# A cross-attention kernel on one core: a new order of all engines and transfers, other softmax forms for seven groups, and the last product, sum and store in halves

## The chip, the core and the metric

The kernel runs on one core of a Trainium2 chip. The engines are TensorE (PE in the profile; its weight loads are PEld), VectorE (DVE), ScalarE (ACT), GpSimd (POOL) and SyncE (SP), which here only issues transfers. Each engine works through its own queue in order, and semaphores hold an instruction until what it needs is done. The metric is the device time of one execution in microseconds (us); the median of three runs before the change is 498.08 (498.07 to 498.1).

## The reference

Everything is float32. With x of 2 batches x 2048 tokens x 640 channels, and a context of 2 x 154 tokens x 1024 channels, of which 77 are text and 77 image prompt:

```python
q = _split_heads(hidden_states @ Wq.T, H)          # 20 heads of 32
k = _split_heads(text @ Wk.T, H)
v = _split_heads(text @ Wv.T, H)
out_text = _merge_heads(_attend(q, k, v, sm_scale))
k_ip = _split_heads(ip @ Wk_ip.T, H)
v_ip = _split_heads(ip @ Wv_ip.T, H)
out_ip = _merge_heads(_attend(q, k_ip, v_ip, sm_scale))
out = out_text + IP_SCALE * out_ip                 # IP_SCALE = 1
out = out @ Wo.T + bo
return out + residual
```

`_attend` is a softmax of the scaled scores times the values. So there are two softmaxes of 77 keys for each token and head, an output projection, and a residual.

## The kernel before

**Tiling.** All inputs come transposed, with the contracted dimension first. The 640 channels are five chunks of 128, of four heads each. Work is numbered by a unit u = 0 to 19, a half (1024 tokens) of one chunk of one batch; q = u // 2 counts batch and chunk, so units 0 to 9 are batch 0 and 10 to 19 batch 1. Within a unit the scores come in three groups s = 0, 1, 2 of three, three and two tiles of 128 tokens. A group's scores lie as rows of 154 (text and image keys side by side), four heads to a tile, in the big buffer `pb`.

**The order by hand.** The function that issues the instructions does nothing but walk a string of words, `SCHEDULE`, in order (before 1024 words, now 1031). Each word puts its instructions at the end of the queues of the engines that it uses, so the order of the words is the order on each engine; the framework only adds the semaphores. `@n` in a word names the PSUM bank or buffer to use. The words that matter below, with their engine and line before the change:

- `q.u.h`, `cq.u.h`: queries of 512 tokens (PE, L201) and their copy out (ACT, L211). `k`, `v`, `ck`, `cv`: the same for keys and values (PE, L142).
- `R s.u`: the scores of a group (PE, L233). `K`: copy to `pb` (ACT, L245). `M`: row maxima (DVE, L281, or L284 from the bank). `S`: subtract them (POOL, L295). `E`: exponential (ACT, L301 in one piece, L269 row by row). `D`: row sums (DVE, L306). `I`: reciprocal (DVE, L311). `N`: normalise (POOL, L316). `T`: transpose by 32x32 blocks (DVE, L323). `A.q`: weights times values (PE, L332), `CA.q` its copy (ACT).
- `m i.x`, `cm i.x`: the output projection of batch 0 in seven products for each 512 tokens x (PE, L490 and L500), and their sums into `acc` (DVE, L515 and L521). Two products share a bank (`m6` uses that of `m1`): the first must be added before the second is written. `o`, `co`, `p`, `z`, `yz`: the last output chunk. `G`: sums of operands for the products (POOL, L431). `SF`, `SS`: fetch and store a part of `acc` (SP).
- Batch 1's output projection is a scheme of 33 products. `V.w.j.e` is a step of the sum of weights w (L828 or L826), `X.w.e` a sum of tokens (L834), each on DVE (e = d) or POOL (e = p). `F m.h`: product m for the 512 tokens h (PE, L848). `Y c.h.t`: adds what lies in the bank of chain c into an output part (DVE, L792 for the first, L794 after), and after the part's last add its store is issued (SP, L798).
- `LX`, `LQ`, `LK`, `LW`, `LA`: loads (SP).

**Softmax forms.** A plain group takes K, M, S, E, D, I, N, T. A group in `BIASED` has no S: the exponential runs row by row, 24 or 16 times, with the negated maximum as bias. A group in `DIRECT` also has no K: maxima and exponential read the banks. A group in `SUMMED` has no D: each row's exponential also sums, and each such sum costs a read instruction on ScalarE.

Of the kernel before, what the change touches and what calls it, by code (L numbers as in the profile page):

```python
# [9 lines left out]
F32 = mybir.dt.float32  # L10
# [10 lines left out]
def kernel(  # L21
# [25 lines left out]
    nc = tc.nc  # L47
    P = 128
# [16 lines left out]
        (11, 0), (13, 0), (13, 2), (14, 0), (14, 2), (15, 1), (15, 2), (16, 2), (18, 1),  # L65
    }
    BIASED = {
        (2, 2), (3, 2), (4, 2), (5, 2), (6, 2), (7, 2), (9, 2), (11, 2), (12, 0), (12, 2), (18, 2), (19, 0),
        (19, 2),
    }  # L70
    SUMMED = {
        (4, 2), (6, 2), (11, 2), (12, 0), (12, 2), (13, 0), (13, 2), (14, 0), (15, 1), (15, 2), (18, 1),
        (18, 2), (19, 2),
# [480 lines left out]
    for t in range(2):  # L554
# [233 lines left out]
    def add_part(o, ps, op):  # L788
# [7 lines left out]
        if not parts_left[o]:  # L796
            m, i = o
            nc.sync.dma_start(out=outT[ts(m, P), ds(S + i * TB, TB)], in_=t)  # L798
# [92 lines left out]
```

## Time and profile before

| | |
|---|---|
| median of three runs | 498.08 us |
| profiled execution: span | 496.7 us |
| busy: PE, DVE, ACT, POOL | 490.3, 408.5, 315.0, 362.5 us |
| granted TensorE clock | 1.00 in every stage |
| DMA | 69.38 MB, 140 GB/s in the mean |

The profiled execution's span runs from its first to its last recorded instruction; a run's time is some 1.4 us longer than this span. A row of a timeline gives its start, its length, engine, line, operation, output and inputs, shapes and how many instructions were joined, and in brackets how long the engine had been idle and what released it. A row of a group gives busy time, mean ns of one, and the idle time before.

### The profile page before, as it was taken

To read this page: it belongs to the slowest core of one execution; us is meant where nothing else is said; L and a number is where in the kernel's file an instruction comes from. 1 tells how busy PE (TensorE), PEld (TensorE's weight loads), DVE (VectorE), ACT (ScalarE), POOL (GpSimd) and SP (SyncE) were. 2 spreads that over 40 slices of the span, in tenths; PEclk is the share of its full clock that TensorE was granted. 3 is DMA by queue.
4 is the path that set the end of the run, shared out by engine and by line. 5 is a ranking of instruction groups with operands and counts; after the bars stand their busy time and mean duration, and the time that the engine had idled before them with its cause. 6 is when DMAs were issued, how large, how long until landed. Compare 5 with 4: busy or idle time off the path is not lost.

```text
span 496.7 us, 10482 instructions
## 1 busy us (share of the span) xinstructions
PE 490.3 (99%) x4114; PEld 287.9 (58%) x4114; DVE 408.5 (82%) x412; ACT 315.0 (63%) x1021; POOL 362.5 (73%) x157
## 2 busy tenths in 40 slices
PE   8999999999999999999999999999999999999997
PEld 5676657657547556456647654755755675444442
DVE  0069989979979989969976896687999978898877
ACT  1165878978978778668999786587578966100000
POOL 0069978798888999989874858565899888284830
PEclk9999999999999999999999999999999999999999
DMA  8991440332360454886445177418525401420115
GB/s 259 356 246 40 132 120 1 106 93 69 92 213 3 132 178 132 274 273 237 158 152 191 58 244 210 133 57 246 174 69 171 127 23 43 149 84 1 43 73 223
DMA packets 67474, 69.38 MB, mean 140 GB/s; under 512 B 5473, under 2 KB 47201, under 8 KB 67425
## 3 DMA queue, kind: packets, MB, share of 16 engines
q1 hardware_dynamic: 66704, 68.00, 43.8%
q8 instruction: 32, 0.52, 0.5%
q10 hardware_dynamic: 720, 0.72, 0.4%
q14 instruction: 18, 0.14, 0.1%
HBM read 54.94 MB, written 10.49 MB: 132 GB/s over the span
## 4 chain that ended last, share of the span: by engine, by line
PE 92%; DMA 3%; SPq 1%; DVE 1%; POOL 1%; ACT 1%; issue 0%; POOLq 0%
PE bank L201 33%; PE bank L848 11%; PE bank L490 10%; PE bank L233 10%; PE bank L332 10%; PE bank L142 9%; PE bank L471 6%; PE bank L500 3%; DMA aT<-in_L_xattn_Wk_ip_dram 2%; DMA wq<-in_L_xattn_Wq_dram 2%; SPq L534 1%; POOL pb L316 1%; DVE den L306 0%; ACT pb L301 0%; SPq L132 0%
## 5 line engine op out<-in xcount | busy, mean ns | idle before, releaser
L316 POOL TENSOR_TENSOR pb<-pb,rden 128x1848 f32<-128x1848 f32 (+1 forms) x60 | 176.1, 2944 | 39.7 <-DVE rden L311 35.5
L201 PE MATMUL bank<-x,wq 128*128 128x512 f32 x400 | 180.4, 601 | 0.6 <-DMA x<-in_x_dram 0.5
L295 POOL TENSOR_TENSOR pb<-pb,mx 128x1848 f32<-128x1848 f32 (+1 forms) x38 | 119.3, 3152 | 51.8 <-DVE mx L281 51.5
L201 PEld LDWEIGHTS bank<-x,wq 128*128 128x128 f32 x400 | 74.1, 191 | 86.7 <-issue 80.8
L323 DVE STREAM_TRANSPOSE pb<-pb 128x1920 f32<-128x1920 f32 (+1 forms) x60 | 115.7, 1932 | 4.9 <-POOL pb L316 4.3
L281 DVE TENSOR_REDUCE mx<-pb 128x24 f32<-128x1848 f32 (+1 forms) x51 | 93.7, 1850 | 30.7 <-ACT pb L245 30.5
L245 ACT COPY pb<-bank 128x462 f32<-128x462 f32 (+1 forms) x204 | 87.2, 539 | 36.0 <-PE bank L233 35.4
L306 DVE TENSOR_REDUCE den<-pb 128x24 f32<-128x1848 f32 (+1 forms) x47 | 88.7, 1895 | 17.6 <-ACT pb L301 13.3
L301 ACT ACTIVATE pb<-pb 128x1848 f32<-128x1848 f32 (+1 forms) x38 | 64.2, 1696 | 17.8 <-POOL pb L295 17.5
L269 ACT ACTIVATE pb<-pb,mx 128x77 f32<-128x77 f32 x224 | 67.8, 364 | 0.3 <-DVE mx L281 0.2
L233 PEld LDWEIGHTS bank<-kT,qT 32*128 32x128 f32 x1280 | 45.4, 184 | 26.9 <-issue 15.6
L269 ACT ACTIVATE pb<-bank,mx 128x77 f32<-128x77 f32 x184 | 51.8, 386 | 9.3 <-DVE mx L284 9.3
L233 PE MATMUL bank<-kT,qT 32*128 32x154 f32 x1280 | 56.2, 305 | 0.3 <-ACT kT L559 0.3
L332 PE MATMUL bank<-pb,v 32*32 32x512 f32 x1600 | 55.2, 597 | 0.0
L142 PE MATMUL bank<-wo_ct,aT 128*128 128x154 f32 x320 | 45.6, 296 | 0.3 <-DMA aT<-in_L_xattn_Wk_ip_dram 0.3
L142 PEld LDWEIGHTS bank<-wo_ct,aT 128*128 128x128 f32 x320 | 42.9, 188 | 3.6 <-issue 2.2
L332 PEld LDWEIGHTS bank<-pb,v 32*32 32x32 f32 x1600 | 29.9, 103 | 22.8 <-issue 10.7
L211 ACT ACTIVATE qT<-bank 128x512 f32<-128x512 f32 x40 | 24.2, 619 | 22.1 <-PE bank L201 22.0
L471 PE MATMUL bank<-aT,wo_ct 128*128 128x512 f32 x80 | 36.1, 596 | 0.0
L269 ACT ACTIVATION_READ_ACCUMULATOR pb<-bank,mx 128x1 f32 x128 | 33.6, 267 | 0.0
L490 PE MATMUL bank<-aT,wo_ct 128*128 128x256 f32 x128 | 32.3, 385 | 0.0
L490 PEld LDWEIGHTS bank<-aT,wo_ct 128*128 128x128 f32 x128 | 23.7, 190 | 6.5 <-issue 3.0
(75 smaller groups left out, 434.4 us busy)
## 6 DMA issues: line engine op xcount, KB each, us to landing
x<-in_x_dram SPq DMA_DIRECT2D x20, 1280.0 KB, 6.7
out_dram<-acc SPq DMA_DIRECT2D x20, 256.0 KB, 2.3
x<-in_x_dram SPq DMA_DIRECT2D x18, 256.0 KB, 5.9
acc<-in_x_dram SPq DMA_DIRECT2D x16, 256.0 KB, 4.7
out_dram<-x SPq DMA_DIRECT2D x15, 256.0 KB, 2.0
v<-vS SPq DMA_DIRECT2D x160, 20.0 KB, 2.8
wq<-in_L_xattn_Wq_dram SPq DMA_DIRECT2D x9, 320.0 KB, 5.0
aT<-in_L_xattn_Wk_dram SPq DMA_DIRECT2D x5, 512.0 KB, 5.5
```

The costliest lines, as they stand in the source:

```text
L142: nc.tensor.matmul(keys_in(out), loaded[n][:, k, :], cT[:, k, :, t, :], start=(k == 0), stop=(k == NCC - 1))
L201: nc.tensor.matmul(pq, wqs[q % 3][:, k, :], xs[place_of(u, h)][:, k, :], start=(k == 0), stop=(k == NC - 1),)
L233: nc.tensor.matmul(ps[g][:, ts(t, 2 * L)], qTs[(u, h)][g * D : (g + 1) * D, ts(st, P)], kT[g * D : (g + 1) * D, c, b].rearrange("p t l -> ...
L245: nc.scalar.copy(keys_of(u, s)[:, :, g], ps[g][:, : n * 2 * L].rearrange("p (n l) -> p n l", n=n))
L269: nc.scalar.activation(row, row if ps is None else rows_in(ps[g], n)[:, t, x], AF.Exp, bias=maxs[(u, s)][:, *one], accum_out=None if den i ...
L281: nc.vector.tensor_reduce(mx, rows_of(u, s), AX.X, ALU.max, negate=negate)
L295: nc.gpsimd.tensor_tensor(rows_of(u, s), rows_of(u, s), maxs[(u, s)].unsqueeze(3).to_broadcast([P, n, 2, L]), ALU.subtract)
L306: nc.vector.tensor_reduce(den_of(u, s), rows_of(u, s), AX.X, ALU.add)
L316: nc.gpsimd.tensor_tensor(rows_of(u, s), rows_of(u, s), rdens[(u, s)].unsqueeze(3).to_broadcast([P, n, 2, L]), ALU.mult)
L323: nc.vector.transpose(p, p)
L332: nc.tensor.matmul(pa[r][g * D : (g + 1) * D, :], v4s[q % 2][rows, g, k, :], zones[rows, :, g, k, :], start=(k == 0), stop=(k == NK - 1),)
L490: nc.tensor.matmul(part, w_of[m][:, kp, op], t_of(m, b, i)[:, kp], start=(op == kp == 0 and m in (1, 2, 5)), stop=(op == 1 and kp == 1 and ...
```

## The change

1. Three sets of forms change. `DIRECT` loses (14, 0) and gains (12, 0); `BIASED` loses (12, 0), (18, 2), (19, 0) and gains (10, 0); `SUMMED` loses (4, 2), (13, 0), (13, 2), (14, 0), (18, 2). Each pair is (unit, group). Gone from the order are S0.10 and K0.12; new are D2.4, D0.13, D2.13, K0.14, S0.14, D0.14, S2.18, D2.18 and S0.19.
2. The whole of `SCHEDULE` is in another order, transfers included.
3. `CLOSING` names product F6.1 and the add Y0.1.10. The product is issued as two matmuls of 256 columns, and the add as two halves, each with its own store.
4. The places of the resident blocks (`home`) are worked out ahead, so that `LA` can stand later in the order.

The diff, cut to its core (of the order, the lines spoken of later):

```diff
     DIRECT = {
-        (11, 0), (13, 0), (13, 2), (14, 0), (14, 2), (15, 1), (15, 2), (16, 2), (18, 1),
+        (11, 0), (12, 0), (13, 0), (13, 2), (14, 2), (15, 1), (15, 2), (16, 2), (18, 1),
     }
     BIASED = {
-        (2, 2), (3, 2), (4, 2), (5, 2), (6, 2), (7, 2), (9, 2), (11, 2), (12, 0), (12, 2), (18, 2), (19, 0),
-        (19, 2),
+        (2, 2), (3, 2), (4, 2), (5, 2), (6, 2), (7, 2), (9, 2), (10, 0), (11, 2), (12, 2), (19, 2),
     }
     SUMMED = {
-        (4, 2), (6, 2), (11, 2), (12, 0), (12, 2), (13, 0), (13, 2), (14, 0), (15, 1), (15, 2), (18, 1),
-        (18, 2), (19, 2),
+        (6, 2), (11, 2), (12, 0), (12, 2), (15, 1), (15, 2), (18, 1), (19, 2),
     }
...
-        "CA.8 G7.3 T2.18 m5.3@0 V.P.0.d K1.19 V.D.0.d V.P.1.d V.I.0.p V.Q.0.d X.B.p@2 m1.3@2 M1.19 V.K.0.p R0.19@1 "
+        "E2.18 D2.18 R1.19@1 V.P.0.d CA.8 m5.3@0 I2.18 SS.2.2 SF.3.2 N1.18 K1.19 SS.3.4 m1.3@3 N2.18 X.B.p@2 V.P.1.d "
+        "V.Q.0.d G6.3 T1.18 SS.2.3 VS.9.0 M1.19 cm5.3 S1.19 T2.18 R0.19@1 K0.19 M0.19 S0.19 E1.19 SF.3.3 m2.3@2 V.T.0.d "
...
+        "F23.0 F26.1@0 F30.0 X.X.p@r31 Y0.0.01 Y6.1.21 F23.1 X.Q.p@10 Y2.1.31 Y2.0.31 V.F.0.p F30.1 F13.0 Y2.1.21 "
+        "Y7.1.21 Y7.0.21 F24.0 F2.1 V.W.1.d F2.0 F15.1 X.O.d@2 Y6.0.20 Y7.1.11 F13.1 F8.0 X.P.p@13 Y7.0.11 X.J.d@4 "
+        "Y6.1.20 X.K.p@1 F5.1 F8.1 Y7.1.31 X.F.p@r21 F5.0 F15.0 Y6.0.30 Y2.1.11 Y7.0.31 F27.1 F27.0 F1.0 Y2.0.11 "
...
+    CLOSING = (6, 1), (0, 1, "10")
+
+    def add_part(o, ps, op, cut=1):
+        whole, n = sum_at(o), TB // cut
+        fresh = o in untouched
+        untouched.discard(o)
+        parts_left[o] -= 1
+        for z in range(cut):
+            add_columns(o, whole[:, ts(z, n)], ps[:, ts(z, n)], op, fresh, z * n)
+
+    def add_columns(o, t, ps, op, fresh, first):
+        if fresh:
             nc.vector.scalar_tensor_tensor(t, t, bo_sb[:, o[0] : o[0] + 1], ps, ALU.add, op)
         else:
             nc.vector.tensor_tensor(t, t, ps, op)
         if not parts_left[o]:
             m, i = o
-            nc.sync.dma_start(out=outT[ts(m, P), ds(S + i * TB, TB)], in_=t)
+            nc.sync.dma_start(out=outT[ts(m, P), ds(S + i * TB + first, t.shape[-1])], in_=t)
...
-            nc.tensor.matmul(
-                at[(c, h)], weight(w), tokens_of(x)[:, h], start=first, stop=True, skip_group_check=True
-            )
+            cut = 2 if (m, h) == CLOSING[0] else 1
+            for z in range(cut):
+                cols = ts(z, TB // cut)
+                nc.tensor.matmul(
+                    at[(c, h)][:, cols], weight(w), tokens_of(x)[:, h, cols], start=first, stop=True,
+                    skip_group_check=True,
+                )
```

How the order moves instructions is shown at three places. In these listings a row is a line, an operation, and its output and inputs; the changed kernel's line numbers differ by a few (L316 is now L314, L323 L321, L281 L279, L515 L513, L828 L829, L826 L827, L834 L835, L794 L798, L848 L852).

**VectorE and GpSimd behind attention A.8.** VectorE before, from I2.18 (T1.18, T2.18, then V.P.0 and V.D.0, V.P.1, V.Q.0, M1.19, cm5.3, cm2.3):

```order
L311 RECIPROCAL rden_2_3506<-den_2_3400 128x16
L323 STREAM_TRANSPOSE pb<-pb 128x1920
L323 STREAM_TRANSPOSE pb<-pb 128x1280
L828 TENSOR_TENSOR pb<-wo_ct 128x128 x2
L828 TENSOR_TENSOR pb<-pb,wo_ct 128x128
L826 SCALAR_TENSOR_TENSOR pb<-pb,wo_ct 128x128
L281 TENSOR_REDUCE mx_1_3554<-pb 128x24
L515 SCALAR_TENSOR_TENSOR acc<-bank_67,bo_sb,acc 128x256 x2
L515 SCALAR_TENSOR_TENSOR acc<-bank_70,bo_sb,acc 128x256 x2
```

VectorE now, from D2.18 (then V.P.0, I2.18, V.P.1, V.Q.0, T1.18, M1.19, cm5.3, T2.18, M0.19, V.T.0):

```order
L304 TENSOR_REDUCE den_2_3488<-pb 128x16
L829 TENSOR_TENSOR pb<-wo_ct 128x128
L309 RECIPROCAL rden_2_3513<-den_2_3488 128x16
L829 TENSOR_TENSOR pb<-pb,wo_ct 128x128
L827 SCALAR_TENSOR_TENSOR pb<-pb,wo_ct 128x128
L321 STREAM_TRANSPOSE pb<-pb 128x1920
L279 TENSOR_REDUCE mx_1_3542<-pb 128x24
L513 SCALAR_TENSOR_TENSOR acc<-bank_67,bo_sb,acc 128x256 x2
L321 STREAM_TRANSPOSE pb<-pb 128x1280
L279 TENSOR_REDUCE mx_0_3564<-pb 128x24
L829 TENSOR_TENSOR pb<-pb,wo_ct 128x128
```

The two transposes have moved from ahead of the weight sums to behind them, I2.18 stands between V.P.0 and V.P.1, and a sum D2.18 is new.

GpSimd before, from N1.18 (N2.18, G7.3, V.I.0, X.B, V.K.0):

```order
L316 TENSOR_TENSOR pb<-pb,rden_1_3417 128x12x154
L316 TENSOR_TENSOR pb<-pb,rden_2_3506 128x8x154
L431 TENSOR_TENSOR aT<-aT 128x2x256
L828 TENSOR_TENSOR pb<-pb,wo_ct 128x128
L834 TENSOR_TENSOR aT<-aT 128x1024
L828 TENSOR_TENSOR pb<-wo_ct,pb 128x128
```

GpSimd now, from S2.18 (N1.18, N2.18, X.B, G6.3, S1.19):

```order
L293 TENSOR_TENSOR pb<-pb,mx_2_3396 128x8x154
L314 TENSOR_TENSOR pb<-pb,rden_1_3480 128x12x154
L314 TENSOR_TENSOR pb<-pb,rden_2_3513 128x8x154
L835 TENSOR_TENSOR aT<-aT 128x1024
L429 TENSOR_TENSOR aT<-aT,x_85 128x2x256
L293 TENSOR_TENSOR pb<-pb,mx_1_3542 128x12x154
```

N2.18 has come from ahead of the weight sums to the row that follows I2.18, the subtraction S2.18 is new, and V.I.0 and V.K.0 have moved to a later place.

**VectorE and GpSimd in the last stage.** VectorE now, from the add Y2.1.21 (Y7.1.21, Y7.0.21, V.W.1, X.O, Y6.0.20, Y7.1.11, Y7.0.11, X.J, Y6.1.20):

```order
L798 TENSOR_TENSOR x_83<-x_83,bank_72 128x512
L798 TENSOR_TENSOR x_83<-x_83,bank_67 128x512
L798 TENSOR_TENSOR x_84<-x_84,bank_74 128x512
L829 TENSOR_TENSOR pb<-pb,wo_ct 128x128
L835 TENSOR_TENSOR aT<-pb 128x1024
L796 SCALAR_TENSOR_TENSOR acc<-acc,bo_sb,bank_68 128x512
L798 TENSOR_TENSOR x_83<-x_83,bank_67 128x512
L798 TENSOR_TENSOR x_84<-x_84,bank_74 128x512
L835 TENSOR_TENSOR pb<-aT 128x1024
```

GpSimd now, from X.L (X.X, X.Q, V.F, X.P, X.K, X.F):

```order
L835 TENSOR_TENSOR pb<-aT,pb 128x1024
L835 TENSOR_TENSOR aT<-aT 128x2x512
L835 TENSOR_TENSOR pb<-aT,pb 128x1024
L829 TENSOR_TENSOR pb<-wo_ct 128x128
L835 TENSOR_TENSOR pb<-pb,aT 128x1024
L835 TENSOR_TENSOR x_85<-aT,pb 128x1024
L835 TENSOR_TENSOR aT<-aT 128x2x512
```

GpSimd before, from X.P (X.L, X.V, X.K, X.Q, V.R.1, X.N):

```order
L834 TENSOR_TENSOR pb<-pb,aT 128x1024
L834 TENSOR_TENSOR pb<-aT,pb 128x1024
L834 TENSOR_TENSOR pb<-aT 128x1024
L834 TENSOR_TENSOR x_85<-aT,pb 128x1024
L834 TENSOR_TENSOR pb<-aT,pb 128x1024
L828 TENSOR_TENSOR pb<-pb,wo_ct 128x128
L834 TENSOR_TENSOR pb<-x_85,pb 128x1024
```

On GpSimd X.P has moved from ahead of X.L to behind X.X and X.Q. On VectorE the weight sum V.W.1 and the token sum X.O now stand back to back ahead of the adds that empty chain 6's banks.

**The end.** TensorE before:

```order
L848 MATMUL bank_71<-pb,wo_ct 128x512
L848 MATMUL bank_73<-pb,wo_ct 128x512
L848 MATMUL bank_67<-aT,pb 128x512
L848 MATMUL bank_67<-pb,wo_ct 128x512
```

TensorE now:

```order
L852 MATMUL bank_67<-aT,pb 128x512
L852 MATMUL bank_67<-pb,wo_ct 128x512
L852 MATMUL bank_73<-aT,pb 128x256 x2
L852 MATMUL bank_73<-pb,wo_ct 128x512
```

VectorE now, its last adds:

```order
L798 TENSOR_TENSOR acc<-acc,bank_67 128x512
L798 TENSOR_TENSOR x_84<-x_84,bank_70 128x512
L798 TENSOR_TENSOR x_82<-x_82,bank_73 128x256 x2
```

The halved product F6.1 stands last but one; the last, F18.1, is whole, and the two half-adds read its bank.

More of the change, by code (lines that the diff above doesn't have):

```diff
@@ L786, in sum_at @@
         return acc[:, m] if m < NC - 1 else res
-    def add_part(o, ps, op):
-        t = sum_at(o)
-        if o in untouched:
-            untouched.discard(o)
+    CLOSING = (6, 1), (0, 1, "10")
[8 more added lines that the diff above has]
+        if fresh:
             nc.vector.scalar_tensor_tensor(t, t, bo_sb[:, o[0] : o[0] + 1], ps, ALU.add, op)
@@ L794, in add_part @@
             nc.vector.tensor_tensor(t, t, ps, op)
-        parts_left[o] -= 1
         if not parts_left[o]:
             m, i = o
-            nc.sync.dma_start(out=outT[ts(m, P), ds(S + i * TB, TB)], in_=t)
-    home = {}
+            nc.sync.dma_start(out=outT[ts(m, P), ds(S + i * TB + first, t.shape[-1])], in_=t)
+    home = {step_of(u)[3] * NH + h: xs[place_of(u, h)] for u, h in late[-XROOM:]}
     def finish(k, args, where):
@@ L809, in finish @@
         elif k == "LA":
-            for u, h in late[-XROOM:]:
-                home[step_of(u)[3] * NH + h] = xs[place_of(u, h)]
             (fourth,) = set(range(NHB)) - set(home)
@@ L847, in finish @@
             w, x = PRODUCTS[m].split()
-            nc.tensor.matmul(
-                at[(c, h)], weight(w), tokens_of(x)[:, h], start=first, stop=True, skip_group_check=True
-            )
+            cut = 2 if (m, h) == CLOSING[0] else 1
[5 more added lines that the diff above has]
+                )
         elif k[0] == "Y":
             c, h, t = int(k[1:]), int(args[0]), args[1]
-            add_part((int(t[0]), NH * int(t[1]) + h), at[(c, h)], sign_of[(c, t)])
+            add_part(
+                (int(t[0]), NH * int(t[1]) + h), at[(c, h)], sign_of[(c, t)], 2 if (c, h, t) == CLOSING[1] else 1
+            )
         else:
```

118 rows, old and new, of the table SCHEDULE are left out of this document.

## The prediction

> **What bounds the kernel now.** I read the page first (busy time, chain of waits), then the table by stages, then the waits of TensorE.
>
> ```profile
> span 496.7 us, 10482 instructions
> PE 490.3 (99%) x4114; PEld 287.9 (58%) x4114; DVE 408.5 (82%) x412; ACT 315.0 (63%) x1021; POOL 362.5 (73%) x157
> ...
> PE 92%; DMA 3%; SPq 1%; DVE 1%; POOL 1%; ACT 1%; issue 0%; POOLq 0%
> ```
>
> TensorE is busy for 490.3 of 496.7 us and carries 92% of the chain that ended last. No other engine is full over the span. The stages say where its missing time lies, and how close the next engine is:
>
> ```profile
> 0.00:24.40 24.40, 22.29 (x76) 13.44 (x76) 0.17 (x1) 3.69 (x8) 0.83 (x6) 1.00 0.96 306
> ...
> 346.30:388.70 42.40, 42.40 (x396) 26.11 (x400) 40.26 (x38) 31.48 (x100) 38.54 (x17) 1.00 0.45 138
> ...
> 442.20:496.70 54.50, 50.80 (x119) 21.93 (x117) 43.83 (x66) 0.00 (x0) 25.23 (x12) 1.00 0.23 87
> ```
>
> The columns are length, PE, PEld, DVE, ACT, POOL, clock, DMA share, GB/s. TensorE idles 2.1 us in the start, which waits for the first loads, and 3.7 us in the last stage, nearly all of it behind its last product. Between them it is full. VectorE has only 2.1 us to spare from 346.30 to 388.70, and that is the engine whose lateness would show next. The waits that the profile names are small:
>
> ```profile
> PE bank L201 <- DMA x<-in_x_dram: 0.5, 1, 0.5
> ...
> PE bank L490 <- DVE acc L515: 0.2, 1, 0.2
> ```
>
> So three things can change the time: TensorE's own work, the small hand-offs inside it, and what stands behind the last product. A new order can win little and lose anything.
>
> **TensorE's work: 0.** Both programs have the same score, query, attention and output products. One of 128x512 becomes two of 128x256, with equal columns. The same groups of scores and of attention stand between the other products, only in another sequence, so I count no work gained or lost.
>
> **Hand-offs: -0.5 (-1.1 to +0.2).** Where TensorE is a little held up, a row is longer than its like, or the gap to it is:
>
> ```profile
> 58.07 1.80 PE L233 MATMUL bank<-kT,qT 32*128 32x154 f32 x40
> ...
> 80.63 1.59 PE L233 MATMUL bank<-kT,qT 32*128 32x154 f32 x40
> ...
> 311.10 1.07 PE L233 MATMUL bank<-kT,qT 32*128 32x154 f32 x24
> 312.41 1.13 PE L490 MATMUL bank<-aT,x 128*128 128x256 f32 x4 [0.24 <-DVE acc L515]
> ...
> 406.42 0.59 PE L500 MATMUL bank<-aT,x 128*128 128x256 f32 x2
> 407.13 1.97 PE L490 MATMUL bank<-aT,x 128*128 128x256 f32 x8
> ```
>
> Forty scores take 1.80 us at 58.07 and 1.59 us at 80.63: 0.21 lost. At 312.41 another 0.24 goes. The two products of 406.42 need about 0.44 by the rate of the row behind them (1.97 for eight), so they are through at 406.86, and the next begin at 407.13: about 0.27 goes. There are ten such places, 2.6 us in all by the same reading. In the new order the scores after q.3.0 have a key or value projection ahead of them, and the row of 312.41 follows other work: these two and a like one go (0.7), and I find two new ones of 0.1 to 0.2 where a projection follows attention. That is -0.5; the bounds are three more gone, and three more new. The hand-off at 407.13 is dealt with below.
>
> **The end in halves: -0.3 (-0.45 to +0.1).**
>
> ```profile
> 493.03 0.69 DVE L794 TENSOR_TENSOR acc<-acc,bank 128x512 f32<-128x512 f32 x1 [0.41 <-PE bank L848]
> 493.75 0.33 SPq L798 DMA_DIRECT2D out_dram<-acc  x1
> ```
>
> ```profile
> out_dram<-acc SPq DMA_DIRECT2D x20, 256.0 KB, 2.3
> ...
> L515 DVE SCALAR_TENSOR_TENSOR acc<-bank,bo_sb,acc 128x256 f32<-128x256 f32 x32 | 13.7, 468 | 7.0 <-PE bank L500 7.0
> ```
>
> Behind the last product stand one add of 0.69, one issue and the flight of 256 KB, some 3.7 us to the end. In the change the product that is cut, F6.1, is the last but one; F18.1 is last and whole and writes the bank that both half-adds read. So the cut of the product gains nothing. The two half-adds cost about 0.4 each (the 256-column add of L515, 0.47, has three operands) in place of 0.69: the second ends 0.1 later, while the first half's store is under way and the last flight carries 128 KB. If half of the flight of 2.3 us were size, it would save 0.6; two issues of 0.33 follow one another and the fixed part stays. I take -0.3, nearer to the issue row than to the size. It costs +0.1 if the flight is all latency.
>
> **The forms: 0.**
>
> ```profile
> L269 ACT ACTIVATION_READ_ACCUMULATOR pb<-bank,mx 128x1 f32 x128 | 33.6, 267 | 0.0
> ```
>
> ```profile
> L306 DVE TENSOR_REDUCE den<-pb 128x24 f32<-128x1848 f32 x35 | 72.1, 2060 | 14.0 <-ACT pb L301 13.3 <-ACT pb L269 0.6
> ...
> L306 DVE TENSOR_REDUCE den<-pb 128x16 f32<-128x1232 f32 x12 | 16.9, 1412 | 3.6 <-ACT pb L269 3.6
> ```
>
> Five groups no longer sum on ScalarE: 96 reads of up to 0.27, some 26 us less there. VectorE gets five sums back, 2 x 2.06 + 3 x 1.41 = 8.4 us over 490. Neither engine is the bound; they lie beside TensorE's products. The cover is thin only where VectorE is nearly full, and there (D2.18, 1.41) T1.18 and T2.18 have been moved behind it. That is the next term.
>
> **The turn of V.Q: +1.4 (0 to +2.4).** Two rows of one stretch show who gets in where VectorE leaves a gap between two sums:
>
> ```profile
> 392.20 2.26 POOL L316 TENSOR_TENSOR pb<-pb,rden 128x1232 f32<-128x1232 f32 x1 [0.42 <-DVE rden L311]
> ...
> 396.46 0.46 POOL L828 TENSOR_TENSOR pb<-pb,wo_ct 128x128 f32<-128x128 f32 x1 [0.77 <-DVE pb L828]
> ```
>
> ```profile
> 396.30 0.28 DVE L828 TENSOR_TENSOR pb<-pb,wo_ct 128x128 f32<-128x128 f32 x1
> 396.61 0.45 DVE L826 SCALAR_TENSOR_TENSOR pb<-pb,wo_ct 128x128 f32<-128x128 f32 x1
> ...
> 472.73 1.50 DVE L828 TENSOR_TENSOR pb<-pb,wo_ct 128x128 f32<-128x128 f32 x1
> ```
>
> ```profile
> 469.41 4.66 POOL L834 TENSOR_TENSOR aT<-aT 128x1024 f32<-128x1024 f32 x2
> ```
>
> V.Q.0 must wait for V.P.1, and in this gap (396.58 to 396.61) GpSimd's V.I.0, asked for at 396.46, got in: V.Q.0 took 0.45, not 0.28. At 472.73 a VectorE sum of 0.28 took 1.50: it ended at 474.23, just behind GpSimd's pair of sums (469.41 + 4.66 = 474.07). So the two engines hold one another out with such two-input instructions. In the new order V.Q.0 has the same gap, but what GpSimd has ready is N2.18, which waits for I2.18, the row before V.P.1. N2.18 is the 2.26 us kind. No row of before has a normalisation against a weight sum: it could hold V.Q.0 for nothing, or for its 2.26 less 0.15. It has the operation and the two SBUF inputs of the sums that do hold, so I take the latter.
>
> The Trainium skill ("SBUF — State Buffer", section "Who interferes with whom") says that a VectorE instruction with two SBUF inputs contends with a GpSimd one that reads SBUF, and whoever issues first has the shared pair for the whole instruction. By it N2.18 holds V.Q.0 too, and the term is the same 1.4; without it the term is 0. The row of 472.73 agrees, with 1.50 for 0.28.
>
> What is late next goes by these rows:
>
> ```profile
> 388.72 5.47 PE bank L332 x153
> ```
>
> ```profile
> 384.77 1.38 DVE L281 TENSOR_REDUCE mx<-pb 128x16 f32<-128x1232 f32 x1
> ...
> 390.43 0.71 DVE L481 SCALAR_TENSOR_TENSOR res<-bank,bo_sb,res 128x512 f32<-128x512 f32 x1
> ```
>
> ```profile
> L316 POOL TENSOR_TENSOR pb<-pb,rden 128x1848 f32<-128x1848 f32 x40 | 131.3, 3288 | 24.8 <-DVE rden L311 22.7 <-ACT aT L355 1.1 <-ACT pb L245 0.6
> ```
>
> ```profile
> L323 DVE STREAM_TRANSPOSE pb<-pb 128x1920 f32<-128x1920 f32 x40 | 86.3, 2160 | 3.7 <-POOL pb L316 3.2
> ...
> L281 DVE TENSOR_REDUCE mx<-pb 128x24 f32<-128x1848 f32 x35 | 71.5, 2051 | 28.4 <-ACT pb L245 28.3
> L323 DVE STREAM_TRANSPOSE pb<-pb 128x1280 f32<-128x1280 f32 x20 | 29.5, 1477 | 1.2 <-POOL pb L316 1.2
> ...
> L521 DVE TENSOR_TENSOR acc<-acc,bank 128x512 f32<-128x512 f32 x12 | 7.9, 662 | 0.8 <-PE bank L490 0.8
> ```
>
> T1.17 must be ready when attention A.8 starts, about 388.4 (388.72 less the hand-offs gone). VectorE being nearly full, I put its end at 387.4 (386.5 to 388.4). Then come co.3 (0.7) and M2.18 (1.4): 389.5. On GpSimd follow S2.18 (2.25, as 392.20), N1.18 (3.29) and, with hops of 0.1 and the row I2.18 between, N2.18 from 395.5 to 397.8; V.Q.0 ends at 398.0. Behind it on VectorE stand T1.18 2.16, M1.19 2.05, cm5.3 2 x 0.47, T2.18 1.48, M0.19 2.05, V.T.0 0.28, cm2.3 2 x 0.47 and cm1.3 0.66: 10.6, less 0.08 of overlap at each of ten: 9.8. cm1.3 ends at 407.8. It empties the bank that m6.3 writes, and m6.3's place on TensorE is 407.13 - 0.27 - 0.5 = 406.4. It is 1.4 late. Without the lost turn V.Q.0 ends 2.1 sooner and m6.3 is on time.
>
> **The turn of V.W.1: +1.8 (0 to +3.9).** In the last stage GpSimd gets four long instructions in a row, X.X, X.Q, V.F, X.P, and then X.K. VectorE comes to V.W.1 and X.O seven adds after F23.0.
>
> ```profile
> L834 DVE TENSOR_TENSOR pb<-aT 128x1024 f32<-128x1024 f32 x7 | 8.3, 1221 | 1.7 <-PE bank L332 1.5 <-ACT aT L359 0.2
> ```
>
> ```profile
> 440.08 0.49 DVE L828 TENSOR_TENSOR pb<-pb,wo_ct 128x128 f32<-128x128 f32 x2
> ...
> 440.13 1.16 POOL L828 TENSOR_TENSOR pb<-wo_ct 128x128 f32<-128x128 f32 x2
> ```
>
> From the end of X.D, X.P is asked for after 2.33 + 2.33 + 0.46 = 5.1 us. F23.0 ends some 0.5 to 1.2 after X.D (my count of the rows between them; both hang on the same adds), and seven adds of 0.6 to 0.7 bring VectorE to V.W.1 after 4.7 to 6.1: mostly behind X.P. Then V.W.1, and X.O, Y6.0.20, Y7.1.11, Y7.0.11, X.J and Y6.1.20 behind it, wait up to 2.3 us, and X.J once more for X.K, which X.O has held out. Y6.0.20 and Y6.1.20 empty the banks of F8.0 and F8.1, ten and twelve products of 0.86 after F23.0. Counted out, with X.O and X.J at 1.2 and adds at 0.6, the slack of 0.9 to 2 us takes part of the first wait and F8.1 is late by about 1.8. If VectorE is first, the cost is 0. If GpSimd's X.K gets in ahead of X.O as well, it is another 2.1, 3.9 in all. The row of 440.08 speaks for the middle: two sums on VectorE back to back kept GpSimd out (two of 0.41 to 0.46 took 1.16).
>
> **Sum:** 0 - 0.5 - 0.3 + 0 + 1.4 + 1.8 = +2.4 on the span of 496.7, so 499.1. The median before, 498.08, is 1.4 above its span, hence **500.5**.
>
> **The rivals.**
> *The turns hold*: normalisation doesn't hold V.Q.0, and V.W.1 comes first. Then -0.8: 497.3. For it: V.W.1 and X.P are within 0.7 us of one another, and nothing shows N against V. Against it: the row of 472.73.
> *Only V.Q's turn is lost*: -0.8 + 1.4: 498.7. For it: the same nearness at V.W.1.
> *X.O's turn goes too*: -0.8 + 1.4 + 3.9 = +4.5: 502.6. By the rule of the Trainium skill named above, X.K, asked for during V.W.1, would come first, which gives this. The row of 440.08 is against it; by that row GpSimd, having asked, was kept out.
> *Transfers late*: stores and fetches of the parts of batch 0 share SP's queue in a new order; the closest fetch has about 2 us in hand, and one of 4.7 us median that misses costs 1 to 2 us: about 499 with no turn lost. DMA is at 0.45 in the busiest of the later stages quoted.
>
> **How the numbers follow.** Forecast 0.30, turns hold 0.27, only V.Q 0.20, X.O too 0.18, transfers 0.05. Less than 0.2%, 1.0 us, can't be told from no change here: faster is below 497.1, slower above 499.1. Turns held spreads from 496.6 to 498.3, half of it faster: 0.14. Same takes its other half, and most of "only V.Q" and of the transfers: 0.32. Slower is the rest, 0.54. The range, 497.0 to 502.8, leaves out half of the faster cases and the worst of the last one; the forecast's own is 499.3 to 501.7.
>
> **What would show it.** Right: V.Q.0 takes over 2 us, and m6.3 begins over 1 us after the product before it; V.W.1 takes over 2 us and F8.1 waits. F18.1 is followed by two adds and two issues, with under 3.7 us to the end. Wrong: V.Q.0 at 0.3 to 0.5 with N2.18 beside it; V.W.1 ahead of X.P; or TensorE idle at a place that I have not named, a product of batch 0 that waits for a fetched part above all.

## The result, and the profile after

The changed kernel takes **502.47 us** (median of four runs, 502.22 to 504.02) where the kernel before took 498.07 beside it: slower by 4.4 us, or by a factor of 1.0088. The ratio on record, 1.0101 with a 95% interval of 1.0085 to 1.0116, is higher, as the mean of the four runs is, with the one of 504.02 among them. The page of the changed kernel, whose span is 500.7 us:

```profile
PE 490.4 (98%) x4116; PEld 287.5 (57%) x4116; DVE 425.8 (85%) x418; ACT 299.9 (60%) x887; POOL 371.6 (74%) x159
...
PE 86%; DVE 7%; DMA 3%; SPq 1%; issue 1%; ACT 1%; POOL 0%; ACTq 0%; DVEq 0%
```

TensorE's own work is the same (490.3 before), and VectorE, which had 1% of the chain that ended last, now has 7%. The table by stages and the waits of TensorE say where:

```profile
388.70:423.70 35.00, 34.66 (x304) 22.83 (x287) 34.01 (x38) 17.52 (x51) 32.38 (x17) 1.00 0.20 60
...
442.20:500.70 58.50, 51.34 (x121) 22.29 (x119) 48.40 (x68) 0.00 (x0) 25.72 (x14) 0.99 0.23 86
```

```profile
PE bank L852 <- DVE acc L796: 2.2, 1, 2.2
PE bank L852 <- DVE x L796: 1.3, 1, 1.3
```

In the last stage TensorE idles 7.2 us (58.50 less 51.34); it was 3.7. The two waits are F8.0 and F8.1. Here is the place, first VectorE (V.W.1, X.O, Y6.0.20), then GpSimd (X.P, X.K), then TensorE (F8.0, F8.1):

```profile
452.99 2.13 DVE L829 TENSOR_TENSOR pb<-pb,wo_ct 128x128 f32<-128x128 f32 x1
455.04 3.36 DVE L835 TENSOR_TENSOR aT<-pb 128x1024 f32<-128x1024 f32 x1
458.32 0.74 DVE L796 SCALAR_TENSOR_TENSOR acc<-acc,bo_sb,bank 128x512 f32<-128x512 f32 x1
```

```profile
452.62 2.36 POOL L835 TENSOR_TENSOR pb<-pb,aT 128x1024 f32<-128x1024 f32 x1
454.92 2.41 POOL L835 TENSOR_TENSOR x<-aT,pb 128x1024 f32<-128x1024 f32 x1
```

```profile
459.12 1.12 PE L852 MATMUL bank<-aT,pb 128*128 128x512 f32 x2 [2.21 <-DVE acc L796]
...
462.42 1.13 PE L852 MATMUL bank<-aT,pb 128*128 128x512 f32 x2 [1.32 <-DVE x L796]
```

V.W.1, alone some 0.28 us, takes 2.13: it ends at 455.12, just behind X.P (454.98). X.O, alone 1.2, takes 3.36: it ends at 458.40, after X.K (457.33) and its own 1.1. X.K had been asked for at 454.92, X.O at 455.04. So both turns were lost.

The other place, VectorE (V.P.0, V.Q.0), GpSimd (N1.18, N2.18) and TensorE (m6.3):

```profile
393.64 0.80 DVE L829 TENSOR_TENSOR pb<-wo_ct 128x128 f32<-128x128 f32 x1
...
394.88 2.27 DVE L827 SCALAR_TENSOR_TENSOR pb<-pb,wo_ct 128x128 f32<-128x128 f32 x1
```

```profile
391.00 3.29 POOL L314 TENSOR_TENSOR pb<-pb,rden 128x1848 f32<-128x1848 f32 x1
394.75 2.25 POOL L314 TENSOR_TENSOR pb<-pb,rden 128x1232 f32<-128x1232 f32 x1 [0.46 <-DVE rden L309]
```

```profile
407.21 1.97 PE L488 MATMUL bank<-aT,x 128*128 128x256 f32 x8 [0.34 <-DVE acc L519]
```

V.P.0 ends at 394.44, behind N1.18 (394.29), and V.Q.0 at 397.15, behind N2.18 (397.00). Normalisation does hold VectorE. Yet m6.3 waits only 0.34. The reason stands just before, in attention A.8 (TensorE), where its weight loads find nothing to issue, while SP has sent two transfers of 256 KB at A.8's start:

```profile
387.78 6.47 PE L330 MATMUL bank<-pb,v 32*32 32x512 f32 x160
```

```profile
393.21 0.13 PEld L330 LDWEIGHTS bank<-pb,v 32*32 32x32 f32 x2 [0.81 <-issue]
```

```profile
387.69 0.37 SPq L459 DMA_DIRECT2D acc<-in_x_dram  x1
388.15 0.42 SPq L463 DMA_DIRECT2D out_dram<-res  x1
```

A.8 takes 6.40 us from its start to that of the scores behind it; it took 5.48 before. The end:

```profile
497.11 0.75 DVE L798 TENSOR_TENSOR x<-x,bank 128x256 f32<-128x256 f32 x2 [0.43 <-PE bank L852]
```

So the difference of the two profiled executions is made up as follows:

| stretch | before | after | difference |
|---|---|---|---|
| to the first long scores | 24.41 | 24.00 | -0.41 |
| from there to A.8 | 364.24 | 363.78 | -0.46 |
| A.8 | 5.48 | 6.40 | +0.92 |
| A.8's end to m6.3 | 13.00 | 13.03 | +0.03 |
| m6.3 to the last add | 85.90 | 89.90 | +4.00 |
| last add to the span's end | 3.68 | 3.56 | -0.12 |
| span | 496.71 | 500.67 | +3.96 |

The first row is not the change's doing: over twelve profiles the first long scores began anywhere from 23.04 to 24.41 us, and that did not go by the order. Without it the change costs 4.37, close to the difference of the medians, 4.40. In every execution of which both time and span are on record the time is 1.7 to 1.9 us above the span (502.48 and 500.7 here), not 1.4; so the profile of the kernel before is of an execution of some 498.5 us, 0.4 above its median, by this estimate.

### The profile page after: what moved, and what is told of

Read it like the earlier page. It is cut to its first block, busy times and chain, and to the rows that moved or that the text cites. A ratio compares the mean times of both kernels' runs of the same rounds, so it can differ in the third digit from the quotient of the medians.

```text
span 500.7 us, 10360 instructions
## 1 busy us (share of the span) xinstructions
PE 490.4 (98%) x4116; PEld 287.5 (57%) x4116; DVE 425.8 (85%) x418; ACT 299.9 (60%) x887; POOL 371.6 (74%) x159
## 4 chain that ended last, share of the span: by engine, by line
PE 86%; DVE 7%; DMA 3%; SPq 1%; issue 1%; ACT 1%; POOL 0%; ACTq 0%; DVEq 0%
PE bank L199 32%; PE bank L852 10%; PE bank L231 10%; PE bank L330 10%; PE bank L488 9%; PE bank L140 8%; PE bank L469 6%; PE bank L498 2%; DMA aT<-in_L_xattn_Wk_ip_dram 2%; DVE mx L279 1%; DMA wq<-in_L_xattn_Wq_dram 1%; SPq L532 1%; DVE pb L321 1%; DVE den L304 1%; DVE aT L835 1%
## 5 line engine op out<-in xcount | busy, mean ns | idle before, releaser
L314 POOL TENSOR_TENSOR pb<-pb,rden 128x1848 f32<-128x1848 f32 (+1 forms) x60 | 175.7, 2940 | 29.7 <-DVE rden L309 23.4
L293 POOL TENSOR_TENSOR pb<-pb,mx 128x1848 f32<-128x1848 f32 (+1 forms) x40 | 125.0, 3131 | 57.0 <-DVE mx L279 56.7
L279 DVE TENSOR_REDUCE mx<-pb 128x24 f32<-128x1848 f32 (+1 forms) x51 | 93.8, 1850 | 31.3 <-ACT pb L243 31.0
L321 DVE STREAM_TRANSPOSE pb<-pb 128x1920 f32<-128x1920 f32 (+1 forms) x60 | 114.6, 1923 | 1.5 <-POOL pb L314 1.2
L304 DVE TENSOR_REDUCE den<-pb 128x24 f32<-128x1848 f32 (+1 forms) x52 | 97.3, 1875 | 18.0 <-ACT pb L299 12.9
L299 ACT ACTIVATE pb<-pb 128x1848 f32<-128x1848 f32 (+1 forms) x40 | 67.4, 1686 | 24.7 <-POOL pb L293 24.6
L267 ACT ACTIVATE pb<-bank,mx 128x77 f32<-128x77 f32 x184 | 48.3, 389 | 10.5 <-DVE mx L282 10.5
L267 ACT ACTIVATE pb<-pb,mx 128x77 f32<-128x77 f32 x184 | 52.8, 374 | 1.8 <-DVE mx L279 1.8
L852 PE MATMUL bank<-aT,pb 128*128 128x512 f32 (+1 forms) x50 | 23.4, 579 | 3.5 <-DVE acc L796 2.2
```

The source lines that it names most:

```text
L267: nc.scalar.activation(row, row if ps is None else rows_in(ps[g], n)[:, t, x], AF.Exp, bias=maxs[(u, s)][:, *one], accum_out=None if den i ...
L279: nc.vector.tensor_reduce(mx, rows_of(u, s), AX.X, ALU.max, negate=negate)
L293: nc.gpsimd.tensor_tensor(rows_of(u, s), rows_of(u, s), maxs[(u, s)].unsqueeze(3).to_broadcast([P, n, 2, L]), ALU.subtract)
L304: nc.vector.tensor_reduce(den_of(u, s), rows_of(u, s), AX.X, ALU.add)
L314: nc.gpsimd.tensor_tensor(rows_of(u, s), rows_of(u, s), rdens[(u, s)].unsqueeze(3).to_broadcast([P, n, 2, L]), ALU.mult)
L321: nc.vector.transpose(p, p)
```

## The experiments

All are variants of the changed kernel unless they say otherwise. Each diff shows the words of the order on the one engine that moves.

**Both turns of the last stage given back (e1).**

```diff
 GpSimd
-X.L X.X X.Q V.F X.P X.K X.F X.N
+X.L X.P X.X X.Q V.F X.F X.K X.N
```

> The changed kernel with two token sums moved on GpSimd alone: X.P from behind V.F to right behind X.L, where GpSimd was idle from 442.30 to 447.58 us, and X.K from right behind X.P to behind X.F. Theory (the loss of the last stage is two lost turns): V.W.1 and X.O find GpSimd idle and take 0.3 and 1.2 us instead of 2.13 and 3.36, F8.0 and F8.1 do not wait (2.21 + 1.32 us before), and 3.5 to 4 us come back: 498.4 to 499.0 us. Rival (VectorE is simply full of adds there and would be late anyway): the two rows get shorter, but TensorE still waits before F8.0 or F8.1 and less than 1 us comes back, 501.5 to 502.5 us.

498.35 us, ratio to before 1.0009 (1.0000 to 1.0019). VectorE's V.W.1 and X.O, and GpSimd's X.P in its new place:

```profile
453.02 0.28 DVE L829 TENSOR_TENSOR pb<-pb,wo_ct 128x128 f32<-128x128 f32 x1
453.22 1.22 DVE L835 TENSOR_TENSOR aT<-pb 128x1024 f32<-128x1024 f32 x1
```

```profile
442.28 2.36 POOL L835 TENSOR_TENSOR pb<-pb,aT 128x1024 f32<-128x1024 f32 x1
```

VectorE has the same rows in the same order at the same time, and they take 0.28 and 1.22. F8.0 and F8.1 do not wait; m6.3 to the last add takes 85.84 (89.90 before this edit). The rival, that VectorE is simply full there, is out: the 4 us were the two turns.

**One turn given back (e2).**

```diff
 GpSimd
-X.X X.Q V.F X.P X.K X.F X.N
+X.X X.Q V.F X.P X.F X.K X.N
```

> Only X.K is moved on GpSimd, to behind X.F; X.P stays. V.W.1 still waits for X.P (2.1 us), but X.O follows it at once, since nothing is ready on GpSimd. Theory: X.O takes 1.2 us in place of 3.36, F8.0 waits 0 to 0.3 us; X.J, two adds later, may then meet X.F, which starts when F13.1 is done, and F8.1 then waits up to 2.5 us: 499.0 us if X.J is ahead of X.F, 501.1 us if not. Rival (the loss is not in X.O's turn): 502.5 us as before.

501.39 us, ratio 1.0073 (1.0052 to 1.0093), the worse of the two cases. VectorE's V.W.1, X.O and X.J, GpSimd's X.F:

```profile
452.61 2.15 DVE L829 TENSOR_TENSOR pb<-pb,wo_ct 128x128 f32<-128x128 f32 x1
454.69 1.21 DVE L835 TENSOR_TENSOR aT<-pb 128x1024 f32<-128x1024 f32 x1
...
457.67 2.37 DVE L835 TENSOR_TENSOR pb<-aT 128x1024 f32<-128x1024 f32 x1
```

```profile
456.61 2.36 POOL L835 TENSOR_TENSOR aT<-aT 128x1024 f32<-128x1024 f32 x1 [2.00 <-PE bank L852]
```

X.O runs at once when nothing is ready on GpSimd. But VectorE is 2 us late by then, so X.J comes while X.F runs (456.61 to 458.97), and F8.1 waits 2.2 us. The lost turn is passed on. This is near to what the forecast took as its likeliest case, with its 1.8 us (there X.J was to wait for X.K, here it waits for X.F); it measured 2.7 (last product's end less m6.3's start, 88.59 for 85.87 before).

**Who has the turn: the first to ask, or GpSimd as long as it has work (e3).** V.W.1 stands ahead of V.W.0 here, so it adds to a sum that is not there yet, and the output leaves that part out; the instructions and their sizes are the same.

```diff
 VectorE
-Y0.1.11 ... Y7.0.21 V.W.1 X.O
+V.W.1 Y0.1.11 ... Y7.0.21 X.O
```

> Only V.W.1 is moved on VectorE, to ahead of the add Y0.1.11, where GpSimd is idle; GpSimd's order is that of the changed kernel. VectorE now comes to X.O at about 453.0 us, while GpSimd runs X.P (to 455.0), and X.K is asked for behind X.P. This tells two rules for the turn apart. Whoever has asked first gets it: X.O, asked for 2 us before X.K, runs at 455.0, ends at 456.2, TensorE hardly waits, and 3.5 to 4 us come back: 498.4 to 499.0 us. GpSimd keeps the turn as long as its next instruction is ready: X.O waits for X.K too, ends at about 458.4 as now, and the time stays within 0.5 us of 502.5.

500.15 us, ratio 1.0046 (1.0031 to 1.0061), between the two. X.O on VectorE, X.K on GpSimd, and m6.3 on TensorE:

```profile
452.04 3.27 DVE L835 TENSOR_TENSOR aT<-pb 128x1024 f32<-128x1024 f32 x1
```

```profile
454.19 3.33 POOL L835 TENSOR_TENSOR x<-aT,pb 128x1024 f32<-128x1024 f32 x1
```

```profile
386.85 5.54 PE L330 MATMUL bank<-pb,v 32*32 32x512 f32 x160
...
406.27 1.97 PE L488 MATMUL bank<-aT,x 128*128 128x256 f32 x8 [1.26 <-DVE acc L519]
```

X.O was asked for at 452.04, waited until X.P was through at 454.2, and ended at 455.31. X.K, asked for at 454.19 as GpSimd's very next instruction, took 3.33 in place of 2.36: it waited for X.O. So GpSimd does not keep the turn as long as it has work, and here the first to ask has it. (That the turn passes to the engine which has not just had it would give the same.) My number was wrong all the same: X.J then met X.K and F8.1 waited 1.3 us. The Trainium skill ("SBUF — State Buffer", section "Who interferes with whom") says that issue order, not shape, decides who blocks; these rows agree, 3.27 with X.O first and 3.36 with X.K first. But it is not shown as a rule for requests that lie close together. In the kernel before, a GpSimd weight sum began 0.04 us ahead of two of VectorE; those took 0.48 together, nothing lost, and it took 0.84 where the like take 0.46:

```profile
427.24 0.84 POOL L828 TENSOR_TENSOR pb<-pb,wo_ct 128x128 f32<-128x128 f32 x1 [3.51 <-DVE pb L828]
```

```profile
427.28 0.48 DVE L828 TENSOR_TENSOR pb<-pb,wo_ct 128x128 f32<-128x128 f32 x2
```

This profile shows something else too. A.8 took 5.47 us here, and m6.3 waited 1.26, not 0.34.

**V.Q's turn given back (e4).**

```diff
 VectorE
-D2.18 V.P.0 I2.18 V.P.1 V.Q.0 T1.18
+D2.18 V.P.0 V.P.1 V.Q.0 I2.18 T1.18
```

> Only V.P.1 and V.Q.0 are moved on VectorE, to ahead of I2.18, so that N2.18 cannot start before V.Q.0 has begun. Theory (N2.18 took V.Q.0's turn): V.Q.0 takes 0.3 us in place of 2.27, all of VectorE's chain to cm1.3 comes about 2 us sooner and m6.3 does not wait. TensorE had lost 0.93 us inside attention A.8 just before, in the one profile of the changed kernel, for a reason that the profile does not name: if that comes again, 0.3 us is gained (502.1 to 502.3 us), if not, about 1.0 to 1.3 (501.1 to 501.5). The other 3.5 us at F8.0 and F8.1 stay. Rival (normalisation does not hold VectorE; V.Q.0 waited for something else): V.Q.0 stays at about 2 us.

501.49 us, ratio 1.0074 (1.0057 to 1.0091). V.Q.0 on VectorE, and m6.3:

```profile
394.05 0.29 DVE L827 SCALAR_TENSOR_TENSOR pb<-pb,wo_ct 128x128 f32<-128x128 f32 x1
```

```profile
406.07 1.99 PE L488 MATMUL bank<-aT,x 128*128 128x256 f32 x8
```

V.Q.0 takes 0.29 and m6.3 does not wait, so N2.18 was the cause. A.8 took 6.48 in this profile, and A.8's end to m6.3 12.62 us for 13.03. That is the 0.4 which was left to win there. The median is 1.0 lower, but the runs of the kernel before beside it are 0.4 lower too (497.68 for 498.07), so some 0.6 is won. With the earlier runs this closes the account of V.Q:

| profile | code fetch ends after A.8's start | A.8 | m6.3 waits |
|---|---|---|---|
| changed kernel | 4.01 | 6.40 | 0.34 |
| e1 | 3.82 | 6.28 | 0.46 |
| e2 | 3.94 | 6.17 | 0.57 |
| e3 | 2.70 | 5.47 | 1.26 |
| e4 (turn given back) | 4.16 | 6.48 | none |
| kernel before | 2.60 | 5.48 | 0.12 (406.42 + 0.59 to 407.13) |

In the first four rows the excess of A.8 over 5.47 and the wait of m6.3 add up to 1.26 or 1.27. With the turn lost, VectorE is ready for m6.3 1.26 us late, and what A.8 has lost already comes off that.

**What A.8 waited for (e5, e9).** The trace has two queues of instruction transfers; the one that carries more is taken to be TensorE's, which has 8232 of the changed kernel's 10360 instructions. On it the next 16 KB of code arrived 2.2 to 2.7 us after A.8's start where A.8 took 5.5 us, and 3.8 to 4.3 us after it where A.8 took 6.2 to 6.5. A first variant had all three turns given back and the cut moved to the last product:

```diff
 GpSimd as in e1, VectorE as in e4
-    CLOSING = (6, 1), (0, 1, "10")
+    CLOSING = (18, 1), (0, 1, "10")
```

> The changed kernel with three edits: X.P behind X.L and X.K behind X.F on GpSimd, V.P.1 and V.Q.0 ahead of I2.18 on VectorE, and the cut moved from product F6.1 to F18.1, the one whose bank the two half-adds read. Theory (the loss was the lost turns, and the end is worth more when the last product is the one that is cut): no wait at F8.0, F8.1 or m6.3. From the end of the last product to the end of the span 3.72 us before and 3.59 in the changed kernel; now the first half-add and its store lie beside the second half of the product, the second store leaves 0.34 us sooner, so 3.25. With the hand-offs (0.46 us before attention A.8): 0.5 + 0.1 + 0.35 = 0.9 us under the kernel before, less up to 1.0 that attention A.8 loses in some profiles of this order: 496.7 to 497.8 us where the kernel before takes 497.7. Rival (the order costs more than the turns): 498 us or more, as the variant with the last stage mended alone (498.35).

497.56 us, ratio 0.9996 (0.9986 to 1.0007); no wait at m6.3, F8.0 or F8.1, and A.8 at 6.53, with the fetch at 4.26. A second variant also moved two words on SP's queue:

```diff
 SP
-SS.2.2 SF.3.2 SS.3.4 SS.2.3 VS.9.0
+SS.2.2 SS.2.3 SF.3.2 SS.3.4 VS.9.0
```

> The run with all turns given back and the last product cut, with one more edit: on SP's queue the fetch SF.3.2 and the store SS.3.4 (256 KB each), which left at 387.5 and 388.0 us, just as attention A.8 began, are moved behind the store SS.2.3, which leaves at about 391.5. So far A.8 took 5.47 us where TensorE's own code fetch ended within 2.7 us of its start, and 6.17 to 6.53 where it ended 3.8 us or more after it, with these two transfers in flight ahead of it. Theory (the moved transfers delay the code fetch and that holds A.8): A.8 takes 5.45 to 5.5 us, all behind it comes 1.0 us sooner, 496.6 us where the kernel before takes 497.7. Rival (A.8 is held by something else, or the fetch is late whatever the transfers): A.8 stays at 6.2 to 6.5 and the time at that of the run without this edit, 497.6.

**496.91 us**, ratio 0.9986 (0.9977 to 0.9995): a little faster than both kernels. SP's queue (SS.2.2 and SS.2.3 joined, SF.3.2) and A.8:

```profile
383.59 8.45 SPq L465 DMA_DIRECT2D out_dram<-acc  x2
392.13 0.42 SPq L459 DMA_DIRECT2D acc<-in_x_dram  x1
```

```profile
387.80 5.55 PE L330 MATMUL bank<-pb,v 32*32 32x512 f32 x160
```

With the two transfers out of the way the fetch ended 2.21 us after A.8's start, and A.8 took 5.48. Beside their own runs of the kernel before, e5 was 0.1 us under it and e9 0.7, so it won 0.6 us, not 1.0. With A.8 on time m6.3 waits 0.4 again, because another turn is lost there: VectorE's V.T.0, 0.28 alone, takes 0.90 behind GpSimd's S1.19 (joined with S0.19 in its row). So giving back V.Q's turn takes the wait of m6.3 from 1.26 (e3) to 0.4, not to nothing.

```profile
403.79 0.90 DVE L829 TENSOR_TENSOR pb<-pb,wo_ct 128x128 f32<-128x128 f32 x1
```

```profile
401.24 6.60 POOL L293 TENSOR_TENSOR pb<-pb,mx 128x1848 f32<-128x1848 f32 x2
```

**The end (e5, e6, e7, e10).** In two variants of the kernel before its own last product, add and store were cut (e6), or the add and store alone (e7).

```diff
 the kernel before, with the changed kernel's add_part
+    CLOSING = (32, 0), (4, 0, "20")    # e6
+    CLOSING = None, (4, 0, "20")       # e7
```

> The kernel before, order and forms untouched, with its own last product F32.0 cut in two of 256 columns and its last add and store in halves. Theory: the end of the span comes 0.12 + 0.34 = 0.46 us sooner, 497.2 us where the kernel before takes 497.7. Rival (the flight of the last store is all latency and the second issue costs what is won): within 0.15 us of the kernel before.

> The kernel before with only its last add and store in halves, no product cut: what the changed kernel's end really does. Read from the profile: from the end of the last product to the end of the span 3.59 to 3.60 us, as in the changed kernel, in place of 3.72.

e6 took 497.82 us, ratio 0.9998 (0.9989 to 1.0007). From the end of the last product to the end of the span it was 3.72 us in the kernel before, 3.59 in the changed kernel, 3.59 in e5, 3.61 in e6 and 3.60 in e7. The halves are worth 0.12 us, and cutting the last product adds nothing. In e5, TensorE's last product and VectorE's half-adds:

```profile
491.61 1.03 PE L852 MATMUL bank<-pb,wo_ct 128*128 128x256 f32 x4
```

```profile
492.68 0.75 DVE L798 TENSOR_TENSOR x<-x,bank 128x256 f32<-128x256 f32 x2 [0.44 <-PE bank L852]
```

The first half-add starts behind the whole product, not behind its half. So e10, the faster variant, had each half-add written directly behind its half of the product:

```diff
                 nc.tensor.matmul(
                     at[(c, h)][:, cols], weight(w), tokens_of(x)[:, h, cols], start=first, stop=True,
                     skip_group_check=True,
                 )
+                if cut > 1:
...
+                    add_columns(o, sum_at(o)[:, cols], at[(c, h)][:, cols], sign_of[(c, t)], False, z * TB // cut)
```

> As the run beside it, and the end written in turn: first half of F18.1, half-add and store, second half, half-add and store. In the runs with the cut product followed by both half-adds the first half-add still began behind the whole product, and the end of the span came 3.59 to 3.61 us after it, cut or not. Theory: now the first half-add waits for its own half alone, and the second starts 0.07 us behind the last product instead of 0.34 behind the first: 3.25 us from the end of the last product to the end of the span, 0.35 us less than the run beside it. Rival (the last store's flight does not leave sooner, because its issue waits for the one ahead): 3.5 to 3.6 us.

497.45 us, ratio 0.9993 (0.9984 to 1.0002). Its second half product and second half-add:

```profile
491.26 0.70 PE L852 MATMUL bank<-pb,wo_ct 128*128 128x256 f32 x2 [0.51 <-DVE x L798]
```

```profile
492.00 0.42 DVE L798 TENSOR_TENSOR x<-x,bank 128x256 f32<-128x256 f32 x1 [0.79 <-PE bank L852]
```

The end is 3.10 us behind the last product, as hoped and more, but the second half of the product now waits 0.51 for the first half-add, which reads the same bank. From the start of the last product to the end of the span it is 4.91 us (490.15 to 495.06) where e9 has 4.62. In both ways of writing it the halves in this bank go one after the other. Whether the chip needs that or only the framework's semaphores ask for it was not tried.

**The forms (e8).**

```diff
 the order and the cut of e5, with DIRECT, BIASED and SUMMED of the kernel before
+S0.10 (ahead of E0.10) K0.12 (ahead of M0.12)
-D2.4 D0.13 D2.13 K0.14 S0.14 D0.14 S2.18 D2.18 S0.19
```

> The order of the run with all turns given back, but with the softmax forms of the kernel before: S0.10 and K0.12 are put back directly ahead of E0.10 and M0.12, and the nine words D2.4, D0.13, D2.13, K0.14, S0.14, D0.14, S2.18, D2.18, S0.19 are taken out. The prediction counted the forms as 0, since ScalarE, VectorE and GpSimd lie beside TensorE's products. By that theory it is within 1 us of that run. Rival (order and forms belong together: ScalarE's row by row exponentials of 24 x 0.39 us and as many reads of 0.27 come where the order leaves no room, at units 13, 14 and 18): TensorE waits at scores of unit 13 or 14, at A.6 or at m5.3, 3 to 8 us in all.

506.48 us in one run, 8.9 above e5. The waits of TensorE:

```profile
PE bank L490 <- DVE acc L521: 2.0, 2, 1.5
...
PE bank L233 <- ACT pb L269: 0.8, 1, 0.8
PE bank L332 <- ACT pb L269: 0.8, 1, 0.8
```

TensorE now waits for ScalarE's row by row exponentials (L269), and scores and A.6 lose 1.6, 1.3 and 2.5 us by their lengths. So the old forms do not fit the new order. What the new forms cost in the old order was not tried, and this is a single run.

## Why the prediction was wrong

It had the direction and the two places, and was short by 2 us: +2.4 forecast, +4.4 measured. Its rival "X.O's turn goes too" gave 502.6 with a chance of 0.18; the kernel took 502.47. That it came so close is in part luck: it counted 1.4 at m6.3, where 0.95 came in, and 0.2 too much gain at the end.

- **TensorE's work, 0**: right, 490.4 us for 490.3.
- **Hand-offs, -0.5**: right, -0.46 from the first long scores to A.8, and at the first of the named places: the forty scores of 58.07 took 1.80 and now take 1.59.

```profile
57.63 1.59 PE L231 MATMUL bank<-kT,qT 32*128 32x154 f32 x40
```

- **The end in halves, -0.3**: the right sign, but mis-sized at -0.12. That cutting F6.1 gains nothing was right. The reason I gave, that it is not the last product, was only half of it: cutting the last one gains nothing either (e5, e6).
- **The forms, 0** (eight groups change, not seven as the title has it): right in this order, where no new wait names ScalarE. ScalarE's busy time fell by 15.1 us and VectorE's rose by 17.3; the 26 and 8.4 of the prediction counted the sums alone, and VectorE's rise holds the lost turns too. The reason, that ScalarE and VectorE lie beside TensorE, is not enough: in e8 no engine but TensorE is busy for over 82% of the span, and it loses 9 us.
- **The turn of V.Q, +1.4**: the mechanism is shown. V.Q.0 took 2.27, and m6.3 waits 1.26 when A.8 is on time (e3). In the profiled execution A.8 lost 0.92 for another reason, and m6.3 waited only 0.34 on top of it. The sum counts 0.27 twice: the 1.4 is taken from a place of m6.3 that has the idle 0.27 of before off already, so against the kernel before it is 1.1. It measured 0.95, A.8 and the stretch to m6.3 together.
- **The turn of V.W.1, +1.8**: this is the step that failed. It measured 4.00. I took the row at 440.08, where two VectorE sums in a row kept GpSimd out, to mean that X.O would follow V.W.1 unhindered. What the runs show is that X.K was asked for as soon as X.P was through, 0.12 us ahead of X.O, and went first; X.O took 3.36 in place of 1.2, and F8.0 waited 2.2 us and F8.1 1.3. At 440.13 GpSimd had also begun 0.15 us ahead of VectorE's second sum (440.29) and was kept out all the same; why the two places differ stays open. Even the case that I took as likeliest was too cheap: with X.K out of the way the lost turn at V.W.1, passed on to X.J, costs 2.7 (e2).
- **Transfers late**, a rival at 0.05: priced for a fetched part of the sums that comes late. What came late was TensorE's code, behind two of the moved transfers, 0.92 us. In this kernel it cost almost nothing, since m6.3 would have waited anyway.

## What to carry to other kernels

Where two engines exclude one another, read for each instruction when it is asked for, not when it is due: a short instruction that misses its turn behind a long one is late by the long one's length, and arrives at the next place late as well. Two waits on one path do not add up if the second only needs the same time to pass; a gain at the first may be taken by the second, as 0.92 won at A.8 was by m6.3 (e3). When an order is planned to fit certain forms or costs, each part must be tried in that order: the forms, which the prediction put at nothing, are worth 8.9 us in this one (e8).

## What was not expected of the hardware

TensorE's code comes in transfers of 16 KB, 32 of them in a run. The Trainium skill ("Runtime: NRT & Kernel Launch", section "Instruction fetch mechanics") says that the sequencer fetches the next block while it executes, and that this is mostly hidden. It was hidden in most of this kernel, and not at attention's small instructions in these profiles: A.8 lost 0.7 to 1.06 us in the six profiles where the fetch ended over 3.8 us after its start (the four in the table, e5, and e8), and nothing in the six where it ended within 2.7. In e7, of the order before, a fetch near A.2 ended 6.1 us after A.2's start in place of 3.6, and the scores behind it lost 1.6 us. Loads of x and Wv had been issued some 5 us ahead in both profiles (137.42 and 137.83, 138.58 and 138.99), so they alone do not explain it. TensorE's wait there:

```profile
PE bank L233 <- issue: 1.1, 1, 1.1
```

That moving the two transfers puts A.8 right is shown by e9, twice with e10 (5.48 in both). But they do not make it late every time: in e3 they stand at the same place in SP's queue, and A.8, from 386.85, is on time.

```profile
386.99 0.37 SPq L459 DMA_DIRECT2D acc<-in_x_dram  x1
```

There the first of them left 0.14 us after A.8's start; in the six late profiles it left between 0.34 ahead of it and 0.06 after it. That would fit a fetch that is asked for near A.8's start and stands behind what left before it, but this was not tried. Which of the two transfers does it, and what decides when the fetch is asked for, stays open.
